# The last two output projections of a two-layer attention kernel: the earlier one set behind the last attention with factors from GpSimd, the last one as seven block products

## Chip, cores and metric

The kernel runs on one core of a Trainium2 chip. Times are device microseconds. The median of three runs is given, and one further execution, taken with the hardware profiler, is what the trace shows.

## What is computed

Two layers, each over eight images of 512 channels by 1024 positions, all in 32-bit floats. The second layer takes the first one's output.

```python
def layer(x, gn_scale, gn_bias, qkv_w, qkv_b, proj_w, proj_b):   # GROUPS is 8, then 32
    xn = group_norm(x) * gn_scale + gn_bias
    q, k, v = split(einsum('oc,bcn->bon', qkv_w, xn) + qkv_b)
    attn = softmax(einsum('bhdi,bhdj->bhij', q, k) / sqrt(64))     # 8 heads of 64
    out = einsum('bhij,bhdj->bhdi', attn, v)
    return einsum('oc,bcn->bon', proj_w, out) + proj_b + x
```

## The kernel before

**Units.** The work is cut into 16 units, one for each layer and image; the last is unit 15. A unit makes v, q and k from its normalised image `xn` (512 x 1024, kept as four tiles of 128 rows), runs attention into `ao`, and needs an output projection with residual. Order in the code is the order on each engine: nothing is moved by a scheduler.

**Block products.** Each 512 x 512 by 512 x 1024 product is done with fewer multiplications: both sides are cut into two by two blocks, and seven products of sums of blocks (numbered 1 to 7, in the order 1, 6, 2, 7, 5, 4, 3) replace eight. This is used twice over, so a product has seven outer and seven inner products, 49 pieces of 128x128 by 128x256. The sums of blocks are called factors. Those of the weights come ready from images in HBM; those of the right side are made by `Right` (L194): `mix` makes the four outer factors on VectorE (DVE), `quarter` and `single` the inner ones, on DVE or GpSimd (POOL). `left.outer(k)` is an outer factor of the weights; of block 21 only the difference with block 11 is kept in place.

**Streams.** `Stream` runs the seven inner products of an outer one: pieces on TensorE (PE) into the PSUM pairs `s0`, `s1`, `a0`, `a1`, `seed` copies between banks on ScalarE (ACT), then a `finish` on DVE and a late part (`add_late`) on POOL. The tail of one product is run inside the next (`close`). Successive products take `a0` and `a1` in turn, each with the other's `s`. `ahead` begins a second product with the first; `held` keeps a product back, and `last_two` runs it interleaved with the one behind it, so that no tail is left over. `hook` runs, behind a named product, parts that other work has put there with `at`.

**Order of a unit.** Products of v, q and k are streamed. Then, from unit 1 on, the output projection of the unit before (`project`, "the old projection") runs as a fourth stream, and then attention. Under v, q and k the last pair of the unit before is finished: sums over partitions by a DVE transposition and reduction, four small DMAs (`lt`), a reciprocal, a DMA out and two broadcast back (`rb`), a division, a bias on ACT. The inner factors of `ao` are made on DVE and POOL in the k stage (`o_part`).

**Attention.** 64 steps of scores, exponential on ACT, product with v, and a running sum of exponentials on DVE, in eight chunks. Parts for the next unit are called from `at_step`; POOL's factors there (`shadows`) follow a named sum, so that they run beside DVE operations with one input. The last unit has no next one, so its attention carries none.

**The end.** Unit 15's projection (`project_last`, L822) is not in blocks: eight groups of four matmuls of 128x512, three of each four first, then the last pair's finish and the check (`verdict`), then the fourth matmul of each group, an addition with bias and residual on DVE, and a store. The residual is loaded into `xn` under the old projection. A flag is written behind it; every engine loads it and branches past a general path that does not run here. All loads and stores here are issued by SyncE (SP), which takes them in order and waits at each for what it needs.

Of the kernel before, what the change touches and what calls it, by code (L numbers as in the profile page):

```python
# [18 lines left out]
P = 128  # L19
# [13 lines left out]
def fast_path(ctx, tc, x, qkv_wT, proj_wT, vecs, groups, out, flag):  # L33
# [43 lines left out]
    abank = [apair[i // 2][:, i % 2, :] for i in range(4)]  # L77
    turns = [t[:, i, :] for i in range(2) for t in (*sbank, *apair)]

# [61 lines left out]
    def block_rows(t, r, h):  # L141
        return t[2 * r * P : 2 * (r + 1) * P, ts(h, FD)].rearrange("(i p) n -> p i n", p=P)
# [265 lines left out]
    def run(steps):  # L408
        for step in steps:
            step()  # L410
# [200 lines left out]
    def make_pairs(stream, w, sel, bias, left, early, hook):  # L611
# [32 lines left out]
        for k in ORDER:  # L644
            if k == 1 and early is not None:
                continue

            def finish(main, m, late, k=k):
                steps[k](main, m, late)
                hook(sel, k)  # L650

            held = k == 4 and sel == "k" and w.u == 0
            stream.product(left.quarters(k), w.right.inner[k], k == 3, finish, held=held)
# [42 lines left out]

    def project(stream, w, left, hook):
        l, b = units[w.u]
# [4 lines left out]

        def load(r, h):
            room, tag = {(1, 0): (rbpool, "rb"), (0, 1): (tmppool, "tmp")}.get((r, h), (ppool, "p"))
            t = res[r, h] = room.tile([P, 2, FD], F32, tag=tag, name=f"res{r}{h}_{w.u}")
            nc.sync.dma_start(t, block_rows(src, r, h))
# [47 lines left out]
        def product(k):  # L755
            def finish(main, m, late):
                steps[k](main, m, late)
                hook("o", k)

            stream.product(left.quarters(k), w.right_o.inner[k], k == 3, finish, held=k == 4)  # L760

# [59 lines left out]

    def project_last(w, wproj, rest):  # L822
        l, b = units[w.u]
        dst = mid[b] if l == 0 else out[b]

        def products(g, c):
            o, h = divmod(g, NH)
            nc.tensor.matmul(  # L828
                turns[g], wproj[:, c, ts(o, P)], ao[:, c, ts(h, FD)],
                start=(c == 0), stop=(c == CC - 1),  # L830
            )

        for g in range(CC * NH):
            for c in range(CC - 1):
                products(g, c)
        for part in rest:
            part()
        for g in range(CC * NH):
            o, h = divmod(g, NH)
            products(g, CC - 1)  # L840
            cols = xn[:, o, ts(h, FD)]
            nc.vector.scalar_tensor_tensor(
                cols, turns[g], vec[:, l, PB, o : o + 1], cols, ALU.add, ALU.add
            )
            nc.sync.dma_start(dst[o * P : (o + 1) * P, ts(h, FD)], cols)

    def attention(w, at_step):
# [79 lines left out]
        def evacuate(c):  # L929
            pr, qh = divmod(c, NH)  # L930
            banks = banks_of(c)
            tmp = tmps[:, c % 2, :]
            if c == n_chunks - 1 and not final:
                i0 = nc.vector.tensor_copy(tmp, banks[0])
            else:
                i0 = nc.scalar.copy(tmp, banks[0])  # L936
            i1 = nc.vector.tensor_add(ao[:, pr, ts(qh, FD)], banks[1], tmp)  # L937
            state["free"][c % 2] = [i0, i1]
# [44 lines left out]
        def divide(pr):  # L983
            col = u * CC + pr
            nc.vector.scalar_tensor_tensor(
                ao[:, pr, :], ao[:, pr, :], 1.0, state["rb"], ALU.mult, ALU.mult,
                accum_out=asum[:, col : col + 1],
            )

        def add_bias(pr, h):  # L990
            cols = ao[:, pr, ts(h, FD)]
# [81 lines left out]
    for u in range(2 * B):  # L1073
        w = Unit()
        w.u, w.right, w.last, w.ready = u, right, {"v": []}, {}
        w.v = vpool.tile([P, NT, C], F32, tag="v", name=f"v_{u}")
# [4 lines left out]
        def at(sel, k, *parts):  # L1081
            hooks.setdefault((sel, k), []).extend(parts)
# [84 lines left out]
        else:  # L1167
# [15 lines left out]
            def o_part(k, lo=0, hi=4):  # L1183
                return lambda: run(o_parts[k][lo:hi])

# [33 lines left out]
        if u:  # L1219
            at("q", 1, *(partial(load_image, l, "k", 0, k) for k in ORDER))  # L1220
            lo = units[old.u][0]
            for k in ORDER:
                at("q", k, partial(load_image, lo, "o", 1, k))
        ahead = u if last else u + 1
        at("k", 5, partial(load_xn, ahead, 0, 2))
        make_pairs(stream, w, "q", QB, lefts["q"], early["q"], hook)
        if u:
            product = project(stream, old, left_slots[1], hook)
            at("k", 4, partial(old.load_res, 0, 0))
            at(  # L1230
                "k", 3, partial(load_xn, ahead, 2), partial(old.load_res, 1, 0), partial(old.load_res, 1, 1),
                partial(old.load_res, 0, 1),
            )
            at("o", 1, partial(stats_of, 0, 1))
            at("o", 2, partial(stats_of, 2, 3))
            at("o", 7, partial(stats_of, 4, 5))
            at("o", 3, partial(stats_of, 6, 7))
        else:
            at("k", 3, partial(load_xn, ahead, 2))
        make_pairs(stream, w, "k", KB, lefts["k"], early["k"], hook)  # L1240
        make = MAKE.get(u)
        if make is not None:
            at("o", 7, partial(load_raw, *make, left_slots[0]))
        if u:
            for k in ORDER:
                product(k)
        wproj = None
        if last:
            wproj = slots[0].rearrange("p k o -> p (k o)")[:, : CC * C].rearrange("p (c o) -> p c o", c=CC)
            nc.sync.dma_start(wproj, proj_wT[1].rearrange("(c p) o -> p c o", p=P))  # L1250

        right = Right(xn, xt) if not last else None
        mixing = {}
        if not last:
# [21 lines left out]
            def rest_of_high(right=right):  # L1276
                xb = ppool.tile([P, 2, FD], F32, tag="p", name=f"xb_{u + 1}")
                room, kept = halves(xb)
                run(right.quarter((2, 3), (*halves(spare), room), nc.gpsimd, kept)[1 if u == 0 else 2 :])

        making = [] if last else [None] * 8
        if make is not None:
            making = [part for parts_of in mix_left(left_slots[0]) for part in parts_of]

        def at_step(s, state):
            if nxt is None:
                return
            c, t = divmod(s, NT)
            st, stats, aggregate, means, variances, scales, apply, _ = nxt
# [323 lines left out]
```

## Time and profile before

| | us |
|---|---|
| median of three runs (lowest, highest) | 3172.73 (3171.10, 3173.76) |
| the profiled execution | 3174.36 |
| its span, first to last instruction | 3172.5 |
| PE busy in the span | 3157.8 |
| attention of unit 15 | 3028.41 to 3138.44 |
| last projection on PE | 3138.44 to 3166.10 |

The parts of a profile used here: the share of the span of each engine; the list of waits (engine and line, what it waited for, us in total, times, longest); tables of stretches with the busy time of each engine; and the timeline, with start, duration, engine, line and operation. L445 is a piece of a streamed product, L882 and L910 are scores and products of attention, L828 the last projection, L716 and L554 additions on POOL, L927 the running sums on DVE. Two instructions of PE make one matmul of 32-bit floats.

### The profile page before, as it was taken

What the parts mean: (1) busy time and instruction counts of PE and PEld (TensorE: products, weight loads), DVE (VectorE), ACT (ScalarE), POOL (GpSimd) and SP (SyncE); (2) the same over time, 40 slices, a digit from 0 to 9 for tenths busy, and PEclk for the clock granted to TensorE, in tenths of its full rate; (3) what the DMA queues carried; (4) which work ended last, traced back from release to release, by engine and by line L of the source; (5) the groups of instructions that cost most, each with busy time, mean ns of one, the idle gap of its engine ahead of it and who ended that gap; (6) DMA issues with size and microseconds to landing.
All of it is one profiled execution on the core that took longest, in us unless ns stands there. A gap on an engine that the chain in (4) does not pass through costs nothing.

```text
span 3172.5 us, 63788 instructions
## 1 busy us (share of the span) xinstructions
PE 3157.8 (100%) x24276; PEld 2023.4 (64%) x24276; DVE 2689.3 (85%) x3151; ACT 2040.3 (64%) x3572; POOL 1265.1 (40%) x966
## 2 busy tenths in 40 slices
PE   9999999999999999999999999999999999999999
PEld 7466494765847658476584756748567485674843
DVE  7988989889798897888979888798897988879777
ACT  3666767667676666766667666676666766667664
POOL 5245272452715427053361533615336162351610
PEclk9999999999999999999999999999999999999999
DMA  4334342433434324233142331423314232243311
GB/s 176 106 123 141 115 157 95 158 129 115 162 110 143 122 63 168 74 120 128 57 168 79 124 118 57 168 80 133 108 57 174 87 129 101 72 164 92 137 53 50
DMA packets 155559, 365.82 MB, mean 115 GB/s; under 512 B 30192, under 2 KB 45808, under 8 KB 155248
## 3 DMA queue, kind: packets, MB, share of 16 engines
q1 hardware_dynamic: 154528, 360.98, 34.0%
q8 instruction: 197, 3.23, 0.4%
q14 instruction: 114, 0.93, 0.1%
q10 hardware_dynamic: 720, 0.68, 0.1%
HBM read 299.72 MB, written 59.77 MB: 113 GB/s over the span
## 4 chain that ended last, share of the span: by engine, by line
PE 95%; DVE 3%; issue 1%; DMA 1%; SPq 0%; ACT 0%; POOL 0%; DVEq 0%; POOLq 0%; ACTq 0%
PE a L910 26%; PE s L882 25%; PE s L445 23%; PE a L445 17%; DVE acc L927 1%; PE a L882 1%; PE s L828 0%; PE a L828 0%; PE a L410 0%; DVE w L410 0%; DVE tr L942 0%; PE s L345 0%; PE s L410 0%; DMA lt<-red 0%; SPq L956 0%
## 5 line engine op out<-in xcount | busy, mean ns | idle before, releaser
L890 ACT ACTIVATE p<-s 128x1024 f32<-128x1024 f32 x976 | 998.1, 1024 | 516.8 <-PE s L882 490.9
L910 PE MATMUL a<-p,v 64*64 64x512 f32 x8192 | 1098.7, 589 | 0.0
L882 PE MATMUL s<-q,k 64*64 64x512 f32 x7808 | 1057.0, 590 | 1.3 <-POOL k L554 1.3
L927 DVE TENSOR_TENSOR acc<-acc,p 128x1024 f32<-128x1024 f32 x768 | 956.2, 1245 | 75.0 <-ACT p L890 33.0
L454 ACT COPY a<-s 128x256 f32<-128x256 f32 x1728 | 615.2, 358 | 345.8 <-PE s L445 246.3
L910 PEld LDWEIGHTS a<-p,v 64*64 64x64 f32 x8192 | 381.6, 131 | 497.7 <-ACT p L890 351.4
L882 PEld LDWEIGHTS s<-q,k 64*64 64x64 f32 x7808 | 380.8, 133 | 435.7 <-issue 435.7
L459 ACT COPY late<-s 128x256 f32<-128x256 f32 x432 | 161.1, 373 | 199.9 <-PE s L445 185.9
L445 PE MATMUL s<-k,w 128*128 128x256 f32 x672 | 195.2, 379 | 0.5 <-ACT a L454 0.5
L927 DVE TENSOR_TENSOR acc<-p,p 128x1024 f32<-128x1024 f32 x128 | 156.2, 1221 | 10.1 <-ACT p L890 10.1
L1327 POOL TENSOR_TENSOR k<-xn 128x256 f32<-128x256 f32 x15 | 11.0, 734 | 374.3 <-PE s L882 298.2
L942 DVE STREAM_TRANSPOSE tr<-acc 128x1024 f32<-128x1024 f32 x128 | 158.1, 1235 | 0.0
L950 DVE TENSOR_REDUCE red<-tr 128x32 f32<-128x1024 f32 x128 | 154.2, 1204 | 0.0
L445 PE MATMUL a<-xn,w 128*128 128x256 f32 x492 | 146.4, 379 | 0.0
L445 PE MATMUL a<-xt,w 128*128 128x256 f32 x462 | 137.4, 379 | 0.0
L445 PEld LDWEIGHTS s<-k,w 128*128 128x128 f32 x672 | 125.0, 190 | 19.2 <-ACT a L454 1.3
L303 POOL TENSOR_TENSOR y<-var,half 128x4 f32<-128x4 f32 (+1 forms) x17 | 18.7, 1097 | 284.7 <-DVE var L301 284.7
L937 DVE TENSOR_TENSOR ao<-a,tmp 128x512 f32<-128x512 f32 x128 | 88.1, 688 | 49.4 <-ACT tmp L936 48.8
L554 POOL TENSOR_TENSOR q<-q,late 128x512 f32<-128x512 f32 x64 | 99.4, 1553 | 63.2 <-ACT a L454 45.7
L445 PE MATMUL s<-xn,w 128*128 128x256 f32 x372 | 110.7, 379 | 0.0
L445 PE MATMUL s<-xt,w 128*128 128x256 f32 x372 | 110.6, 379 | 0.0
L563 POOL TENSOR_TENSOR v<-v,late 128x512 f32<-128x512 f32 x60 | 89.9, 1499 | 47.1 <-DVE v L665 33.9
(259 smaller groups left out, 5119.4 us busy)
## 6 DMA issues: line engine op xcount, KB each, us to landing
w<-iq SPq DMA_DIRECT2D x105, 448.0 KB, 3.5
w<-ik SPq DMA_DIRECT2D x105, 448.0 KB, 7.0
w<-io SPq DMA_DIRECT2D x105, 448.0 KB, 6.9
w<-iv SPq DMA_DIRECT2D x98, 448.0 KB, 3.7
rb<-drec SPq DMA_DIRECT2D x128, 256.0 KB, 3.8
xn<-mid SPq DMA_DIRECT2D x36, 512.0 KB, 3.6
res<-x_dram SPq DMA_DIRECT2D x32, 512.0 KB, 5.9
mid<-res SPq DMA_DIRECT2D x32, 512.0 KB, 2.8
```

What stands on the lines that cost most here:

```text
L445: nc.tensor.matmul(to, at, moving, start=start, stop=j != 1, skip_group_check=True),
L454: n = nc.scalar.copy(dst, one)
L459: on("ACT", nc.scalar.copy(late, seventh), s, 1)
L554: return nc.gpsimd.tensor_add(cols, cols, twice(late))
L563: return nc.gpsimd.tensor_add(cols, cols, parts)
L882: nc.tensor.matmul(bank[e * H : (e + 1) * H, j, :], w.k[pr][j * H : (j + 1) * H, t * P + e * H : t * P + (e + 1) * H], w.q[pr][j * H : (j ...
L890: exp = nc.scalar.activation(p, bank, AF.Exp, scale=SCALE)
L910: nc.tensor.matmul(banks[r][j * H : (j + 1) * H, :], w.v[rows, t, lo : lo + D], p[rows, j, :], start=(t == 0), stop=(t == NT - 1),)
L927: state["sums"].append(nc.vector.tensor_add(acc, state["first"] if t == 1 else acc, p))
L937: i1 = nc.vector.tensor_add(ao[:, pr, ts(qh, FD)], banks[1], tmp)
L942: nc.vector.transpose(tr, state["acc"].pop(c))
L950: nc.vector.tensor_reduce(red[:, :, qh, :], state["tr"].rearrange("p j (f i) -> p j f i", i=BL), AX.X, ALU.add)
```

## The change

Four things change, all in unit 15.

- Its old projection, that of unit 14, runs behind its attention and no longer before it. The last two products of k are interleaved instead (`held`), the first two of the moved projection are begun together (`ahead`), and its last two are no longer interleaved. The finish of unit 15's last pair hangs on the products of the moved projection.
- The inner factors of `ao` for it are made by POOL, in 16 parts at 14 steps of the last attention, in the weight slot that k has left; the parts on DVE and POOL in the k stage are dropped. Its residuals go to `xt` and `spare`.
- Unit 15's attention writes into `xn` instead of `ao`. One more DVE subtraction (`again`, 128x896) at step 3 restores a block of the weights.
- The last projection is seven outer products of four matmuls of 128x512 each, with sums on DVE, ACT and POOL. Its residuals go to q's tiles, loaded once attention is over. The flag's matmul stands before its last product.

The core of the diff; the residual load in `project`, `evacuate`, `divide` and `add_bias` change only in the tile that they name:

```diff
@@ -649,7 +648,7 @@
-            held = k == 4 and sel == "k" and w.u == 0
+            held = k == 4 and sel == "k" and w.u in (0, 2 * B - 1)
             stream.product(left.quarters(k), w.right.inner[k], k == 3, finish, held=held)
@@ -702,6 +701,10 @@
         def load(r, h):
+            if rooms is not None:
+                res[r, h] = rooms[r, h]
+                nc.sync.dma_start(res[r, h], block_rows(src, r, h))
+                return
             room, tag = {(1, 0): (rbpool, "rb"), (0, 1): (tmppool, "tmp")}.get((r, h), (ppool, "p"))
@@ -757,7 +760,11 @@
-            stream.product(left.quarters(k), w.right_o.inner[k], k == 3, finish, held=k == 4)
+            inner = w.right_o.inner
+            after = (left.quarters(6), inner[6]) if k == 1 and rooms is not None else None
+            stream.product(
+                left.quarters(k), inner[k], k == 3, finish, ahead=after, held=k == 4 and rooms is None
+            )
@@ -819,30 +826,76 @@
-    def project_last(w, wproj, rest):
+    def project_last(stream, w, left, again, rooms, rest, flagged):
...
-        dst = mid[b] if l == 0 else out[b]
-
-        def products(g, c):
-            o, h = divmod(g, NH)
-            nc.tensor.matmul(
-                turns[g], wproj[:, c, ts(o, P)], ao[:, c, ts(h, FD)],
-                start=(c == 0), stop=(c == CC - 1),
+        right = w.right_o
+        add = nc.vector.tensor_add
+        res = {}
+        for (r, h), room in rooms.items():
+            res[r, h] = room
+            nc.sync.dma_start(room, block_rows(source_of(w.u), r, h))
...
+        def steps(bank, k):
+            return [
+                partial(
+                    nc.tensor.matmul, bank[:, i, :],
+                    again[:, k - 1, :] if (c, i) == (0, 1) else left.outer(k)[:, c, ts(i, P)],
+                    right.outer[k][:, c, :], start=c == 0, stop=c == 1, skip_group_check=True,
+                )
+                for i in range(2) for c in range(2)
+            ]
...
+        def sums(name):
+            return accpool.tile([P, 2, FD], F32, tag="acc", name=f"{name}_last")
...
+        def more(r, h, t):
+            nc.gpsimd.tensor_add(res[r, h], res[r, h], t)
...
+        def store(r, h):
+            nc.sync.dma_start(block_rows(out[b], r, h), res[r, h])
...
+        first = steps(sbank[1], 1)
+        run(first[:2])
+        stream.close()
+        run(first[2:])
+        p1 = sums("p1")
+        for i in range(2):
+            nc.scalar.activation(p1[:, i, :], sbank[1][:, i, :], AF.Identity, bias=vec[:, l, PB, i : i + 1])
+        more(0, 0, p1)
+        right.mix(1)
+        run(steps(apair[0], 5))
+        right.mix(3)
+        for i in range(2):
+            for t in (res[0, 1], res[1, 1]):
+                add(t[:, i, :], apair[0][:, i, :], t[:, i, :])
+        run(steps(sbank[0], 6))
+        right.mix(2)
+        u2 = sums("u2")
+        add(u2, sbank[0], p1)
+        more(0, 1, u2)
+        run(steps(apair[1], 7))
+        u3 = sums("u3")
+        for i in range(2):
+            nc.vector.scalar_tensor_tensor(
+                u3[:, i, :], apair[1][:, i, :], step_vec[:, l, PB, i : i + 1], u2[:, i, :], ALU.add, ALU.add
...
-
-        for g in range(CC * NH):
-            for c in range(CC - 1):
-                products(g, c)
-        for part in rest:
-            part()
-        for g in range(CC * NH):
-            o, h = divmod(g, NH)
-            products(g, CC - 1)
-            cols = xn[:, o, ts(h, FD)]
-            nc.vector.scalar_tensor_tensor(
-                cols, turns[g], vec[:, l, PB, o : o + 1], cols, ALU.add, ALU.add
-            )
-            nc.sync.dma_start(dst[o * P : (o + 1) * P, ts(h, FD)], cols)
+        more(1, 0, u3)
+        more(1, 1, u3)
+        store(1, 1)
+        run(steps(sbank[1], 2))
+        add(res[0, 0], sbank[1], res[0, 0])
+        store(0, 0)
+        rest()
+        run(steps(apair[0], 4))
+        add(res[1, 0], apair[0], res[1, 0])
+        store(1, 0)
+        flagged(apair[1])
+        run(steps(sbank[0], 3))
+        for i in range(2):
+            t = res[0, 1][:, i, :]
+            add(t, sbank[0][:, i, :], t)
+            nc.sync.dma_start(out[b][i * P : (i + 1) * P, FD:], t)
@@ -930,11 +983,11 @@
             tmp = tmps[:, c % 2, :]
-            if c == n_chunks - 1 and not final:
+            if c == n_chunks - 1:
                 i0 = nc.vector.tensor_copy(tmp, banks[0])
...
                 i0 = nc.scalar.copy(tmp, banks[0])
-            i1 = nc.vector.tensor_add(ao[:, pr, ts(qh, FD)], banks[1], tmp)
+            i1 = nc.vector.tensor_add(w.ao[:, pr, ts(qh, FD)], banks[1], tmp)
             state["free"][c % 2] = [i0, i1]
@@ -1023,12 +1076,10 @@
-        if final:
-            run([partial(add_bias, CC - 2, h) for h in range(NH)] + w.sums)
         w.finish = [partial(reciprocals, CC - 1), partial(divide, CC - 1)]
...
         w.before = [partial(divide, CC - 2), *(partial(add_bias, CC - 2, h) for h in range(NH))]
-        w.right_o = Right(ao, ot)
+        w.right_o = Right(w.ao, ot if not final else w.v[:, :6, :].rearrange("p (a b) o -> p a b o", b=2))
@@ -1181,13 +1232,13 @@
             def o_part(k, lo=0, hi=4):
-                return lambda: run(o_parts[k][lo:hi])
+                return lambda: run(o_parts[k][lo:hi]) if not last else None
...
             at("v", 4, reciprocals, bias_2[0])
-            at("v", 3, bias_2[1], o_rooms, partial(ro.mix, 0))
+            at("v", 3, bias_2[1], *(() if last else (o_rooms,)), partial(ro.mix, 0))
             at("q", 6, divide)
@@ -1221,14 +1272,19 @@
                 at("q", k, partial(load_image, lo, "o", 1, k))
-        ahead = u if last else u + 1
-        at("k", 5, partial(load_xn, ahead, 0, 2))
+        if not last:
+            at("k", 5, partial(load_xn, u + 1, 0, 2))
         make_pairs(stream, w, "q", QB, lefts["q"], early["q"], hook)
-        if u:
+        if last:
+            places = [(0, 0), (0, 1), (1, 0), (1, 1)]
+            product = project(
+                stream, old, left_slots[1], hook, dict(zip(places, (*(xt[:, i] for i in range(3)), spare)))
+            )
+        elif u:
             product = project(stream, old, left_slots[1], hook)
...
             at(
-                "k", 3, partial(load_xn, ahead, 2), partial(old.load_res, 1, 0), partial(old.load_res, 1, 1),
+                "k", 3, partial(load_xn, u + 1, 2), partial(old.load_res, 1, 0), partial(old.load_res, 1, 1),
                 partial(old.load_res, 0, 1),
@@ -1236,18 +1292,14 @@
         else:
-            at("k", 3, partial(load_xn, ahead, 2))
+            at("k", 3, partial(load_xn, u + 1, 2))
         make_pairs(stream, w, "k", KB, lefts["k"], early["k"], hook)
...
             at("o", 7, partial(load_raw, *make, left_slots[0]))
-        if u:
+        if u and not last:
             for k in ORDER:
                 product(k)
-        wproj = None
-        if last:
-            wproj = slots[0].rearrange("p k o -> p (k o)")[:, : CC * C].rearrange("p (c o) -> p c o", c=CC)
-            nc.sync.dma_start(wproj, proj_wT[1].rearrange("(c p) o -> p c o", p=P))
@@ -1278,14 +1330,39 @@
+        else:
...
+            w.ao = xn
+            room = slots[0].rearrange("p k o -> p (k o)")
+            wide = [room[:, i * FD : (i + 1) * FD].rearrange("p (i n) -> p i n", i=2) for i in range(9)]
+            narrow = [room[:, i * FD2 : (i + 1) * FD2].rearrange("p (i n) -> p i n", i=1) for i in range(18, 21)]
+            again = room[:, 21 * FD2 : 21 * FD2 + 7 * P].rearrange("p (k o) -> p k o", k=7)
+            ro = old.right_o
+            fives, fours = (
+                ro.quarter(pair, rooms, nc.gpsimd)
+                for pair, rooms in (((5, 6), wide[3:6]), ((4,), narrow))
+            )
+            wides = [*ro.quarter((1, 7), wide[:3], nc.gpsimd), *fives, *ro.quarter((2, 3), wide[6:], nc.gpsimd)]
+            places = (8, 10, 16, 18, 24, 26, 32, 34, 40, 42, 48, 50)
+            shadows = {s: [part] for s, part in zip(places, wides)}
+            shadows[56], shadows[58] = fours[:3], fours[3:]
+            for r in range(2):
+                for h in range(2):
+                    old.load_res(r, h)
...
         making = [] if last else [None] * 8
...
         def at_step(s, state):
+            c, t = divmod(s, NT)
             if nxt is None:
+                for part in shadows.get(s, ()):
+                    follows(part(), state["sums"][-1 if t == 0 else -2], "beside operations with one input")
+                if s == 3:
+                    quarters = (left_slots[1].block[:, :, i : i + P] for i in (0, P))
+                    nc.vector.tensor_sub(again, *quarters)
                 return
-            c, t = divmod(s, NT)
             st, stats, aggregate, means, variances, scales, apply, _ = nxt
@@ -1344,9 +1421,24 @@
-    project_last(old, wproj, [*old.finish, verdict])
-    nc.tensor.matmul(turns[0][:1, :1], both, ones[:, :1], start=True, stop=True)
-    nc.scalar.copy(flag, turns[0][:1, :1])
...
+    (reciprocals, divide, *bias), (transposed, reduced), (_, *bias_2) = w.finish, w.sums, w.before
+    at("o", 1, transposed, bias_2[0])
+    at("o", 6, reduced, bias_2[1])
+    at("o", 2, partial(w.right_o.mix, 0))
+    at("o", 7, reciprocals)
+    at("o", 3, divide, *bias)
...
+    def flagged(bank):
+        nc.tensor.matmul(bank[:1, 0, :1], both, ones[:, :1], start=True, stop=True)
+        nc.scalar.copy(flag, bank[:1, 0, :1])
...
+    for k in ORDER:
+        product(k)
+    project_last(
+        stream, w, left_slots[1], again,
+        {(r, h): q_pairs[r][:, :, ts(h, FD)] for r in range(2) for h in range(2)}, verdict, flagged,
+    )
```

More of the change, by code (lines that the diff above doesn't have):

```diff
@@ L77, in fast_path @@
     abank = [apair[i // 2][:, i % 2, :] for i in range(4)]
-    turns = [t[:, i, :] for i in range(2) for t in (*sbank, *apair)]
     vec = const.tile([P, 2, 6, CC], F32, name="vec")
@@ L695, in stream_values, with project @@
             stream.product(left.quarters(k), w.right.inner[k], k == 3, finish, True, after)
-    def project(stream, w, left, hook):
+    def project(stream, w, left, hook, rooms=None):
         l, b = units[w.u]
@@ L985, in divide @@
             nc.vector.scalar_tensor_tensor(
-                ao[:, pr, :], ao[:, pr, :], 1.0, state["rb"], ALU.mult, ALU.mult,
+                w.ao[:, pr, :], w.ao[:, pr, :], 1.0, state["rb"], ALU.mult, ALU.mult,
                 accum_out=asum[:, col : col + 1],
@@ L990, in add_bias @@
         def add_bias(pr, h):
-            cols = ao[:, pr, ts(h, FD)]
+            cols = w.ao[:, pr, ts(h, FD)]
             nc.scalar.activation(
@@ L1074, in fast_path @@
         w = Unit()
-        w.u, w.right, w.last, w.ready = u, right, {"v": []}, {}
+        w.u, w.right, w.last, w.ready, w.ao = u, right, {"v": []}, {}, ao
         w.v = vpool.tile([P, NT, C], F32, tag="v", name=f"v_{u}")
```

## The prediction

> **What bounds the kernel now.** I read the share of the span per engine first, then the engine's waits, then a table of stretches, then the timeline around the two seams that the change opens. TensorE (PE) is busy 3157.8 us of the 3172.5 us span at full granted clock, and its waits are few:
>
> ```profile
> PE 3157.8 (100%) x24276; PEld 2023.4 (64%) x24276; DVE 2689.3 (85%) x3151; ACT 2040.3 (64%) x3572; POOL 1265.1 (40%) x966
> PE s L445 <- ACT a L454: 2.2, 3, 1.3
> PE s L882 <- POOL k L554: 1.3, 1, 1.3
> ```
>
> So a gain must come from fewer matmuls or a shorter end, and a loss from a new wait of PE or a longer end. The stretches below are the attention of the last but one unit, that of the last, the old projection before it, the last projection, and what follows PE (columns: length, then busy time of PE, weight loads, DVE, ACT, POOL, then clock, DMA share, GB/s):
>
> ```profile
> 2832.33:2942.59 110.26, 110.26 (x1033) 49.89 (x1032) 98.49 (x114) 76.45 (x84) 17.80 (x18) 1.00 0.28 89
> 3028.41:3138.44 110.03, 110.03 (x1026) 40.49 (x1025) 94.19 (x97) 71.11 (x76) 3.23 (x3) 1.00 0.13 41
> 3006.00:3028.40 22.40, 22.40 (x104) 19.25 (x102) 12.99 (x15) 13.35 (x38) 18.83 (x12) 1.00 0.36 129
> 3138.44:3166.10 27.66, 27.66 (x68) 12.07 (x64) 14.77 (x26) 3.15 (x5) 0.00 (x0) 1.00 0.20 68
> 3166.10:3172.50 6.40, 0.19 (x3) 0.09 (x2) 0.75 (x2) 0.15 (x1) 0.00 (x0) 0.83 0.38 136
> ```
>
> PE never stops in the first four. The last pair's chain (sums, four small DMAs, reciprocal, broadcast, division, bias: 3138.4 to 3158.5) fits under three quarters of the last projection. After PE come a DVE addition, a store of 2.0 us, and about 3 us of ending.
>
> **The change, part by part.** (1) *Matmuls.* A matmul is two instructions here. The old projection, 49 products of 128x256 at 0.4315 us (3006.18, 3006.61, 3007.04 in the timeline), is 21.14 us and only moves. The last one has 32 matmuls of 128x512, 64 instructions at 0.4295 us (the chain's 5.15 us for 12), 27.49 us; seven products of four are 28 matmuls, 24.05 us: **-3.44 us**.
>
> (2) *Attention now starts behind the last two products of k, interleaved.* Unit 0 already starts so, and pays twice: 1.33 us on PE at 81.85 (ACT waits for DVE, which is behind with three weight factors), and 1.31 us at 91.76, where the fifth score step waits for POOL's late addition, itself behind a 3.00 us factor at L1086. Neither factor is there in the last unit, whose o-part factors also leave DVE and POOL in the k stage. DVE's last k addition should end 1.4 us after PE, POOL's 2.7 us after; the third step needs the one at 1.7 us, the fifth the other at 5.3 us. One thing is new: 21 products run before this attention instead of 28, so the first scores write the very bank that the last product's ACT copies still read. In the old order that last copy runs 3028.14 to 3028.50 against the first scores at 3028.41. I take **+0.30**; bounds 0 and unit 0's 2.64.
>
> (3) *Factors by POOL inside attention.* Twelve subtractions of 128x512 (1.28 us, rows of L1327) and four of 128x256 (0.73 us): 18.3 us, and one DVE subtraction of 128x896 (1.08 us). The last attention has 110.03 - 94.19 = 15.84 us of DVE idle. The last but one attention holds 17.80 us of POOL work placed the same way, and is only 0.23 us longer, with seven extra PE instructions. I take **+0.05**; bounds 0 and 0.23, with every factor's time added to DVE as a rival below.
>
> [...]
>
> ```profile
> 2971.47 1.22 DVE L587 TENSOR_TENSOR u_q<-a,p_q 128x1024 f32<-128x1024 f32 x1 [1.67 <-ACT a L454]
> 2972.61 1.22 DVE L985 SCALAR_TENSOR_TENSOR ao<-ao,rb 128x1024 f32<-128x1024 f32 x1
> 2972.77 2.19 POOL L554 TENSOR_TENSOR u_q<-u_q,late 128x512 f32<-128x512 f32 x1 [3.85 <-DVE u_q L587]
> ```
>
> DVE keeps its 1.22 us, POOL goes from 1.27 to 2.19.
>
> (4) *Old projection behind attention.* Set t = 0 where attention's last matmul ends. The seam is the one that ends every other unit's attention, where PE goes on without a listed wait: 0. PE finishes at t = 21.1, plus two matmuls of the last projection run before the old one's tail (1.7): its last product ends at 22.9. DVE meanwhile: evacuation and two sums to 3.9 (as after 2942.66), p1 4.5-5.9, transpose to 7.1, u2 8.3, reduction 9.5, product 2's addition 10.9, one factor 12.1, u3 14.1, reciprocal 15.9, four additions of product 5 to 18.4, product 4 to 20.0, product 3 23.1-24.3. The small DMAs land 3.7 us after the reduction (3144.8 to 3148.5), 13.2, before they are asked for; the broadcast lands 5.9 us after the reciprocal (3149.96 to 3155.89), 21.5, before the division: no wait. Division 25.5, two ACT biases (1.33) 26.9, factor 6 (1.22) 28.1.
>
> (5) *Last projection.* PE ends product 1 at 24.6 and product 5 at 28.06; product 6 needs factor 6, so **+0.15**. The flag's small matmul comes before the last product: **+0.20**, both ends near it (0.19 in the old order). PE ends at 21.14 + 24.05 + 0.35 = 45.54, where it ended at 27.66. Attention ends 21.14 - 0.35 = 20.79 us earlier, so PE ends 20.79 + 27.66 - 45.54 = **2.91 us earlier**.
>
> (6) *SP's queue.* The residuals of the last unit, once loaded under attention, go into q's tiles, and their issue stands behind the old projection's stores. SP waits in order, so it waits for POOL:
>
> ```profile
> SPq L719 <- POOL res L554: 180.5, 45, 10.8
> 3022.59 2.37 POOL L716 TENSOR_TENSOR res<-res,u_o 128x1024 f32<-128x1024 f32 x1
> 3008.08 1.41 SPq L707 DMA_DIRECT2D res<-mid  x3
> 3011.00:3014.00 3.00, 3.00 (x16) 2.63 (x15) 1.33 (x3) 1.80 (x5) 1.98 (x2) 1.00 0.96 352
> 3162.00:3164.00 2.00, 2.00 (x6) 0.90 (x5) 1.79 (x3) 0.00 (x0) 0.00 (x0) 1.00 0.84 327
> ```
>
> POOL has, behind each other, four additions of 2.36 us and six of 1.27 us; from p1 on it runs 5.9, 8.3, 9.6, 12.0, 13.2; then 14.1-17.7; then from product 5's end 18.4-22.0, and product 4's late part at 23.3-23.6. So four loads of 512 KB are issued from 23.7 at 0.45 us each. With one store ahead, 2.6 MB at the 352 GB/s above take 7.4 us from 24.9: the last lands at X = 32.3. DVE needs that block for product 5's four additions (0.68 each; the first needs an earlier block): 34.4, then factor 4 (35.6) and u2 (36.8). POOL then adds u2 and twice u3, three times 2.31 us: 43.75. Only then does SP issue the first of five last stores, and the other four stand behind it. 2.1 MB at 327/0.84 = 389 GB/s is 5.4 us, plus 1.6 us until landing (256 KB lands in 2.0, 512 KB in 2.8): 50.8. Without that queue the last half block would land 3.35 us after PE (0.1 + 0.69 + 0.35 + 2.0, as before: 3166.10 to 3169.3 is 3.2), at 48.9. **+1.9 us.** The loads hide under product 5 to 7; if that cover is gone, the verdict on DVE (8.6 us behind X) comes after the flag's matmul wants it at 42.0, that is from X = 33.4, and PE waits too.
>
> **Sum:** -2.91 + 1.9 - 0.05 (the last addition and store, 3.15 for 3.2) = **-1.06 us**: span 3171.4. The profiled execution took 3174.36 us, 1.86 beyond its span and 1.63 above the median of the runs shown, 3172.73; I keep both offsets, so the median becomes **3171.7 us**. Its own range, X between 31 and 33.3, is 3170.4 to 3172.8.
>
> **Rivals.** *The end stays short* (X at 30 or earlier, POOL prompt): the queue's 1.9 us vanish, -2.9, 3169.8. For it: stores alone land in 2.0 us. Against: seven ordered waits. *Late residuals, the slower side:* X moves one for one into the end; from X = 33.3 the gain is gone. [...] For it: DVE is fuller here than in the old place (division, reduction, factors between). Against: DVE's PSUM reads, most of this stage, left POOL at 1.27 and 2.36. *Unit 0's start repeats:* 2.64 for 0.30, 3174.0; against it, both causes are absent. *Factors collide with sums:* +3.5 by the idle account (18.3 + 1.08 - 15.84), 3175.2; against it stands the neighbouring attention. *It does not shorten the work:* the counts show four matmuls fewer, so this needs a wait that I have not found.
>
> **Chances.** Forecast 0.45, short end 0.20, late residuals 0.17, unit 0's start 0.05, collisions 0.06, an unseen wait 0.07. The range 3169.0 to 3177.3 leaves out the unseen wait and a few hundredths below. A difference of 0.2% is 6.3 us, about what a measurement of this kernel tells from no change. Faster by that needs twice the matmuls saved: 0.02. Slower by that needs over 7 us beyond the sum, the unseen wait or a late chain past its bound: 0.08. Within: 0.90.
>
> **What would show it.** Right: 28 matmuls at L409 at 0.86 us each, no wait of PE over 0.5 us, POOL's factors beside attention of 110.0 to 110.3 us, the old projection 21 us, and stores bunched after PE ends. Wrong: PE waiting at the first five score steps, at L444 behind ACT or DVE, or at L409 for a factor; residuals of the last unit landing before t = 30 or after 34; a last store landing within 3.4 us of PE's end.

## The result, and the profile after

| | before | after |
|---|---|---|
| median (lowest, highest) of 20 runs each, us | 3172.61 (3170.79, 3173.86) | 3177.57 (3175.34, 3178.83) |
| the profiled execution, us | 3174.36 | 3177.55 |
| its span, us | 3172.5 | 3175.7 |
| from the start of unit 15's products of v to the end, us | 229.91 | 235.04 |

The change costs 4.96 us: a ratio of 1.0014, 95% interval 1.0008 to 1.0021. By the medians that is +0.16%, under the 0.2% named above, yet the interval leaves 1 out. The last row of the table compares the two profiles without the two microseconds by which their earlier, unchanged parts differ: 3172.5 - 2942.59 and 3175.7 - 2940.66, **+5.13 us**. All later lengths of "unit 15 to the end" are made in this way, from one profiled execution each.

Engines and PE's waits after:

```profile
PE 3155.9 (99%) x24268; PEld 2027.9 (64%) x24268; DVE 2693.6 (85%) x3152; ACT 2039.7 (64%) x3573; POOL 1283.5 (40%) x978
PE s L344 <- DMA xn<-x_dram: 4.6, 1, 4.6
PE a L1433 <- DVE both L1422: 4.3, 1, 4.3
PE s L444 <- ACT a L453: 2.2, 3, 1.3
PE s L935 <- POOL k L553: 1.3, 1, 1.3
```

Eight instructions of PE (four matmuls) are gone, and one wait is new: the flag's matmul (L1433) waits 4.3 us for DVE. The 4.6 us before the first matmul of the program (L344) stand in the kernel before too, which the prediction's list leaves out. The stretches, with columns as before: unit 15's attention; the old projection with six of the seven last products; the wait; the flag's matmul with the last product; what follows PE.

```profile
3005.51:3115.54 110.03, 110.03 (x1025) 46.27 (x1025) 96.32 (x98) 70.95 (x75) 20.95 (x18) 1.00 0.08 24
...
3115.54:3157.81 42.27, 42.27 (x150) 27.54 (x146) 31.62 (x38) 16.07 (x41) 24.76 (x13) 1.00 0.34 113
3157.81:3162.12 4.31, 0.00 (x1) 0.00 (x1) 4.17 (x8) 0.00 (x0) 3.40 (x2) 0.93 0.00 0
3162.12:3168.97 6.85, 6.85 (x10) 2.60 (x10) 1.09 (x1) 0.15 (x1) 0.00 (x0) 0.54 0.61 233
3168.97:3175.70 6.73, 0.00 (x0) 0.00 (x0) 1.29 (x2) 0.00 (x0) 0.00 (x0) 0.71 0.24 86
```

Attention takes 110.03 us as before, now with 20.95 us of POOL beside it. PE is full until the flag. Then it waits for 4.31 us, and the flag and last product take 6.85 us at a clock of 0.54, where the same work takes 0.20 + 3.44 at full clock: 3.2 us more. So +5.13 is made of -2.7 (the work saved on PE, much as predicted), +4.3, +3.2 and +0.3 (6.73 for 6.40 behind PE). The clock in finer stretches:

```profile
3158.00:3162.00 4.00, 0.00 (x0) 0.00 (x0) 3.86 (x8) 0.00 (x0) 3.21 (x2) 0.94 0.00 0
...
3162.00:3164.00 2.00, 1.88 (x4) 0.92 (x5) 1.21 (x2) 0.15 (x1) 0.00 (x0) 0.50 0.96 373
3164.00:3166.00 2.00, 2.00 (x4) 0.86 (x3) 0.00 (x0) 0.00 (x0) 0.00 (x0) 0.50 0.98 377
3166.00:3168.00 2.00, 2.00 (x4) 0.82 (x3) 0.00 (x0) 0.00 (x0) 0.00 (x0) 0.50 0.13 49
3168.00:3170.00 2.00, 0.97 (x2) 0.00 (x0) 0.99 (x2) 0.00 (x0) 0.00 (x0) 0.91 0.00 0
3170.00:3172.00 2.00, 0.00 (x0) 0.00 (x0) 0.30 (x1) 0.00 (x0) 0.00 (x0) 0.95 0.41 152
```

A mean of 0.94 over 4 us, taken as 1.00 and then the 0.50 of the next rows, is 0.12 x 4 = 0.48 us at half clock: by this estimate the fall is at 3161.5, 3.7 us after PE stopped at 3157.81. From then on PE is at 0.50 until 3168.4, although it works again from 3162.1. By the same sum the clock falls once more at 3171.8, behind the last product.

What the flag waited for, the verdict (its operations at L1416 to L1422), is in the timeline of DVE and POOL:

```profile
3146.76 0.69 DVE L871 TENSOR_TENSOR q<-a,q 128x512 f32<-128x512 f32 x1 [1.87 <-DMA q<-mid]
3150.03 1.89 DVE L871 TENSOR_TENSOR q<-a,q 128x512 f32<-128x512 f32 x3 [2.58 <-DMA q<-mid]
...
3154.26 6.96 POOL L853 TENSOR_TENSOR q<-q,u_last 128x1024 f32<-128x1024 f32 x3 [6.37 <-DVE u_last L875]
...
3155.64 1.21 DVE L887 TENSOR_TENSOR q<-s,q 128x1024 f32<-128x1024 f32 x1
3156.77 2.20 DVE L1416 TENSOR_SCALAR fin<-asum 128x64 f32<-128x64 f32 x1
3159.00 0.22 DVE L1418 TENSOR_REDUCE low<-fin 128x1 f32<-128x64 f32 x1
3159.14 2.12 DVE L1420 TENSOR_SCALAR extremes<-extremes 128x64 f32<-128x64 f32 x1
3161.30 0.22 DVE L1421 TENSOR_REDUCE low<-extremes 128x1 f32<-128x64 f32 x1
3161.44 0.18 DVE L1420 TENSOR_SCALAR extremes<-extremes 128x64 f32<-128x64 f32 x1
```

In the kernel before, the whole verdict takes 1.35 us, 3157.16 to 3158.51:

```profile
3157.16 0.20 DVE L1339 TENSOR_SCALAR fin<-asum 128x64 f32<-128x64 f32 x1
...
3157.53 0.18 DVE L1343 TENSOR_SCALAR extremes<-extremes 128x64 f32<-128x64 f32 x1
...
3158.36 0.15 DVE L1345 TENSOR_REDUCE both<-low 128x1 f32<-128x3 f32 x1
```

In the changed kernel DVE waits twice for the residuals (1.87 and 2.58 us), and the verdict's first operation starts at 3156.77, 1.0 us before PE wants the flag. That operation takes 0.20 us in the kernel before and 2.20 us here; the same operation on `extremes` takes 2.12 us and then, with POOL done, 0.18 us. POOL's three additions of 2.32 us end at about 3156.6, 3158.9 and 3161.2; the two slow operations end at 3158.97 and 3161.26. The reductions between them keep 0.22 us.

### The profile page after: what moved, and what is told of

Read it like the earlier page. It is cut to its first block, busy times and chain, and to the rows that moved or that the text cites. A ratio compares the mean times of both kernels' runs of the same rounds, so it can differ in the third digit from the quotient of the medians.

```text
span 3175.7 us, 63791 instructions
## 1 busy us (share of the span) xinstructions
PE 3155.9 (99%) x24268; PEld 2027.9 (64%) x24268; DVE 2693.6 (85%) x3152; ACT 2039.7 (64%) x3573; POOL 1283.5 (40%) x978
## 4 chain that ended last, share of the span: by engine, by line
PE 97%; DVE 2%; DMA 1%; issue 0%; ACT 0%; POOL 0%; SPq 0%; ACTq 0%; DVEq 0%; POOLq 0%
PE a L963 27%; PE s L935 26%; PE s L444 23%; PE a L444 17%; PE a L935 1%; PE s L409 1%; DVE acc L980 0%; PE a L409 0%; DMA q<-mid 0%; DVE w L409 0%; DMA gmat<-groups_dram 0%; DMA rb<-drec 0%; PE s L344 0%; DMA drec<-rec 0%; POOL k L553 0%
## 5 line engine op out<-in xcount | busy, mean ns | idle before, releaser
L553 POOL TENSOR_TENSOR k<-k,late 128x512 f32<-128x512 f32 x64 | 100.0, 1563 | 23.6 <-DVE k L624 11.7
```

The costliest lines, as they stand in the source:

```text
L553: return nc.gpsimd.tensor_add(cols, cols, twice(late))
```

## Experiments

The theory to be tested: three prices in a chain. Late residuals push the verdict into the time in which POOL adds; POOL's additions stop the verdict's small operations; PE's idle time then lowers its clock. The rivals: the queue of stores behind POOL would set the end in any case; or the moved projection itself costs time. Each median is given beside that of the kernel before on the same chip; the first four ran on one chip, the next four on another, the last two on a third. The changed kernel was not measured again beside them, and each interval reaches 2 to 3 us to either side, so a difference of medians from its 3177.57 is rough; the lengths from unit 15 to the end say where the time lies.

**1. The flag behind the last product.**

```diff
+        run(steps(sbank[0], 3))
         flagged(apair[1])
-        run(steps(sbank[0], 3))
```

> The flag's matmul stands behind the last block product instead of before it; nothing else. Theory (late verdict: TensorE waits 4.3 us for the check on VectorE, and comes out of the wait at half its granted clock, so that the last product takes 6.7 us for 3.4): no wait of TensorE over 0.5 us, clock 1.00 through the last product, and 4.5 to 7.5 us less than the changed kernel's 3177.6, about 3172. Rival 1 (the queue of stores at the end binds whatever TensorE does): 3176 or more. Rival 2 (the clock falls at the end by itself): the 4.3 us go, the slow product stays, about 3173.3 with clock 0.5.

Measured: 3175.68 us against 3172.3, ratio 1.0009 (0.9999 to 1.0018), unit 15 to the end 232.29. The wait no longer stands before a product (1.28 us of it are left behind the last one) and the last product runs at full speed. But 1.9 us of the median and 2.75 of the profile came back, where 4.5 to 7.5 were expected. Last product, stores, and two stretches with the DMA's share and rate in the last two columns:

```profile
3158.60 3.60 PE L409 MATMUL s<-xn,w 128*128 128x512 f32 x8
...
3162.60 2.37 SPq L856 DMA_DIRECT2D out_dram<-q  x3
...
3166.31 0.86 SPq L898 DMA_DIRECT2D out_dram<-q  x2
```

```profile
3163.90:3164.90 1.00, 0.00 (x0) 0.00 (x0) 1.00 (x2) 0.01 (x1) 0.00 (x0) 1.00 1.07 410
...
3166.90:3167.90 1.00, 0.00 (x0) 0.00 (x0) 0.00 (x0) 0.00 (x0) 0.00 (x0) 0.50 1.03 381
```

The last product ends at 3162.2 and the span at 3173.9, 11.7 us later instead of the 6.4 of the kernel before. The first three stores are issued from 3162.6, when POOL is done, and fill the DMA engines (share 1.03 to 1.07); the last two stand behind them and land 4.8 us after their issue, for 3.0 in the changed kernel. So the queue that the prediction described is real and is the next limit, but in the changed kernel it is hidden under the slow last product.

**2. The verdict early**, behind the division, before the residuals matter.

```diff
-        rest()
...
-    at("o", 3, divide, *bias)
+    at("o", 3, divide, *bias, verdict)
```

> The check on VectorE stands right behind the last division, where VectorE would wait for ScalarE's biases, instead of behind product 2's addition. Theory: its seven operations take about 1.4 us there, TensorE does not wait at the flag, clock 1.00, about 3172 to 3173 (the stores still stand behind GpSimd's three last additions). Rival (the check is slowed wherever GpSimd adds, and factor 6 is late instead): 3 to 4 us of waiting at product 6, 3176 to 3178.

Measured: 3173.84 us against 3172.3, ratio 1.0006 (0.9997 to 1.0015); 231.50, between the two expectations. The flag waits for nothing. The new place has a POOL addition too, and the verdict pays there:

```profile
3139.21 2.18 POOL L553 TENSOR_TENSOR xt<-xt,late 128x512 f32<-128x512 f32 x1 [0.82 <-DVE xt L715]
...
3140.31 1.14 DVE L1415 TENSOR_SCALAR fin<-asum 128x64 f32<-128x64 f32 x1
```

The operation ends as POOL's does (3141.45 and 3141.39). Factor 6 comes later by this, and PE waits 0.8 us for it at product 6. The stores still stand behind POOL (first issue at 3160.67), so the residuals keep a price without the verdict.

**3. The residuals early**: the same four loads, issued before the moved projection's products and so ahead of its stores in SP's queue. q's tiles are free from there on.

```diff
-            nc.sync.dma_start(room, block_rows(source_of(w.u), r, h))
...
+    rooms = {(r, h): q_pairs[r][:, :, ts(h, FD)] for r in range(2) for h in range(2)}
+    for (r, h), room in rooms.items():
+        nc.sync.dma_start(room, block_rows(source_of(w.u), r, h))
     for k in ORDER:
         product(k)
...
```

> The last unit's four residual loads are issued before the old projection's products, so that they do not stand behind its stores in SyncE's queue. Theory (late residuals start the chain): the loads land some 25 us earlier, product 5's additions wait for no DMA, the check ends about 3 to 4 us earlier, the first of the last stores goes out 4 us earlier; TensorE waits at the flag for under 1.5 us; 3169.5 to 3172. Rival (the check's operations, held up by GpSimd's additions, are enough alone): the wait at the flag is still over 2 us with a fallen clock, 3174 or more.

Measured: 3171.70 us against 3172.3, ratio 0.9999 (0.9990 to 1.0008); 228.71. As expected: against the changed kernel, 5.9 us of median and 6.3 us of profile come back by the place of four loads.

```profile
3145.84 2.48 DVE L870 TENSOR_TENSOR q<-a,q 128x512 f32<-128x512 f32 x4
...
3156.59 1.73 DVE L1415 TENSOR_SCALAR fin<-asum 128x64 f32<-128x64 f32 x1
3158.30 0.89 SPq L855 DMA_DIRECT2D out_dram<-q  x2
```

DVE's four additions of product 5 run without a wait for a DMA. The verdict still meets POOL (1.73 us), but PE waits only 0.69 us and the clock stays at 1.00.

**4. Five matmuls to fill the wait**, into the other half of the flag's bank, before the flag; their result is not used.

```diff
+        for _ in range(5):
+            nc.tensor.matmul(
+                bank[:, 1, :], left_slots[1].outer(3)[:, 0, :P], w.right_o.outer[3][:, 0, :],
+                start=True, stop=True,
+            )
         nc.tensor.matmul(bank[:1, 0, :1], both, ones[:, :1], start=True, stop=True)
```

> Five matmuls of 128x512 into a free bank (4.3 us of work, result unused) before the flag's matmul fill the time in which TensorE waited. Theory (the wait is what lowers the clock): the clock stays 1.00, the last product takes 3.4 us, 3.3 us less than the changed kernel, about 3174.2. Rival (the clock falls for another reason): the last product takes 6.7 us as before, 3177 to 3178.

Measured: 3175.72 us against 3172.3, ratio 1.0011 (1.0002 to 1.0020); 232.75. With useless work the median is 1.85 us under the changed kernel's, which the intervals do not tell apart; the profile, of the fastest of eleven runs, is 2.29 us shorter. PE's idle time before the flag is 0.54 us, and:

```profile
3161.24 0.19 PE L1438 MATMUL a<-ones,both 128*1 128x1 f32 x2 [0.54 <-DVE both L1422]
3161.36 3.70 PE L409 MATMUL s<-xn,w 128*128 128x512 f32 x8
...
3163.00:3165.00 2.00, 2.00 (x5) 0.57 (x3) 0.00 (x0) 0.00 (x0) 0.00 (x0) 1.00 1.05 407
```

The last product starts when the verdict lets it, as in the changed kernel, but at full clock: the flag and the product take 3.82 us (3161.24 to 3165.06) for 6.85. With the wait filled the clock stays at 1.00, and with PE idle for 4.31 us it fell to 0.50: it was the idleness that lowered it here. Of these 3.03 us, 0.53 are lost because the flag comes that much later in this execution, its residuals landing 0.5 us later behind attention, and 0.2 lie behind PE (6.94 us to the end for 6.73).

**5. What 1 to 4 point to**: residuals early as in experiment 3, the verdict between product 5's additions and factor 4, where POOL is idle, and the store of block (1,1) behind that of (0,0).

```diff
         run(steps(sbank[0], 6))
+        rest()
         right.mix(2)
...
-        store(1, 1)
         run(steps(sbank[1], 2))
         add(res[0, 0], sbank[1], res[0, 0])
         store(0, 0)
-        rest()
+        store(1, 1)
```

> Early residual loads as in the third run, the check on VectorE between product 5's additions and factor 4, where GpSimd has nothing to add, and the store of block (1,1) behind that of (0,0). Theory: the check takes about 1.4 us, TensorE waits nowhere over 0.3 us, clock 1.00, and the saving of matmuls shows at last: 2 to 3 us under the kernel before, 3169.5 to 3170.5. Rival (something else at the end still binds, such as GpSimd's additions or the stores): 3171.5 or more, no gain on the third run's 3171.7.

Measured: 3171.24 us against 3173.49, ratio 0.9994 (0.9985 to 1.0003); 227.54, or 2.37 below the kernel before. That is the 2 to 3 us expected, though not the 3169.5 to 3170.5, since the kernel before took longer on this chip. PE no longer waits at the flag, and all of the verdict's operations take their short time:

```profile
3148.71 0.18 DVE L1415 TENSOR_SCALAR fin<-asum 128x64 f32<-128x64 f32 x1
...
3149.06 0.19 DVE L1419 TENSOR_SCALAR extremes<-extremes 128x64 f32<-128x64 f32 x1
```

**6. The move alone**: the moved projection and POOL's factors stay, with early residuals; the last projection is that of the kernel before, 32 matmuls, with its weights loaded where k's products were.

```diff
-    def project_last(stream, w, left, again, rooms, rest, flagged):
+    def project_last(stream, w, wproj, rooms, rest):
...
+        for g in range(CC * NH):
+            for c in range(CC - 1):
+                products(g, c)
+            if g == 0:
+                stream.close()
+                rest()
```

> The move alone: the old projection behind attention with GpSimd's factors, but the last projection as the 32 matmuls of the kernel before, with its check and flag at their old places, its weights and residuals loaded right behind attention. Theory (the move costs nothing, the block form of the last projection brought both the saving and the waits): within 1 us of the kernel before, 3171.5 to 3173.3, no wait of TensorE over 0.5 us. Rival (the move itself costs, through factors on GpSimd or the last pair's chain): 3174 or more, with the wait in the old projection or behind it.

Measured: 3172.08 us against 3173.49, ratio 0.9995 (0.9986 to 1.0004); 230.11 against 229.91. PE has no wait in the moved part, and the whole is 0.2 us longer in the profile: that is what the move and POOL's factors cost.

**7. POOL's last two additions behind the verdict**, the rest as changed. This tests the stop itself.

```diff
-        more(1, 0, u3)
-        more(1, 1, u3)
-        store(1, 1)
...
-        rest()
+        checked = rest()
+        follows(more(1, 0, u3), checked, "behind the check")
+        more(1, 1, u3)
+        store(1, 1)
```

> As the changed kernel, but GpSimd's last two additions come behind the check, so that the check's two slow operations (2.2 and 2.1 us) have no GpSimd operation beside them. Theory (they stand still until a GpSimd addition ends): each takes 0.2 us, the check ends about 4 us earlier, the wait at the flag falls from 4.3 to under 1 us and the clock stays 1.00; the last two stores are later by some 2 us, so 3174 to 3176.5 in all. Rival (they are slow for another reason, say a first use or the operand): 2 us each as before, wait over 3 us, 3178 or more.

Measured: 3174.66 us against 3173.49, ratio 1.0006 (0.9997 to 1.0015); 233.80.

```profile
3156.91 0.18 DVE L1416 TENSOR_SCALAR fin<-asum 128x64 f32<-128x64 f32 x1
3157.03 9.39 SPq L856 DMA_DIRECT2D out_dram<-q  x3
...
3157.27 0.18 DVE L1420 TENSOR_SCALAR extremes<-extremes 128x64 f32<-128x64 f32 x1
```

With the residuals as late as before and the same operations in the same place, 2.20 and 2.12 us become 0.18 and 0.18: POOL's additions were the cause. PE waits 0.86 us instead of 4.31 and keeps its clock (3.70 us for the last product). The additions are only put off, the issue of the three stores takes 9.4 us (SP waits between them), and most of the gain goes back to the end.

**8. Two filling matmuls in place of five.** The diff is that of the fourth, with `range(2)`.

> As the run with the filled wait, but two matmuls in place of five, so that about 2.6 us of the wait remain. Theory (a wait lowers the clock only past some 3 us): the clock stays 1.00 and the last product takes 3.4 to 3.6 us. Rival (any wait near 2 us lowers it): clock 0.5 and over 5 us for the last product.

Measured in a single execution: 3176.04 us; 234.28. The clock fell and the last product took 5.40 us, against the expectation; but the wait came out at 3.05 us and not at 2.6, so the run shows that 3.05 us can be enough, and does not decide between the theory's "some 3 us" and the rival's "near 2".

```profile
3161.84 0.19 PE L1438 MATMUL a<-ones,both 128*1 128x1 f32 x2 [3.05 <-DVE both L1422]
...
3161.97 5.40 PE L409 MATMUL s<-xn,w 128*128 128x512 f32 x8
...
3162.00:3163.00 1.00, 1.00 (x4) 0.60 (x3) 0.94 (x1) 0.15 (x1) 0.00 (x0) 0.74 1.04 403
3163.00:3164.00 1.00, 1.00 (x2) 0.34 (x1) 0.00 (x0) 0.00 (x0) 0.00 (x0) 0.50 1.06 410
3164.00:3165.00 1.00, 1.00 (x2) 0.34 (x1) 0.00 (x0) 0.00 (x0) 0.00 (x0) 0.50 1.04 399
3165.00:3166.00 1.00, 1.00 (x3) 0.42 (x2) 0.00 (x0) 0.00 (x0) 0.00 (x0) 0.56 0.85 326
```

By the same sum as above (0.74 is 0.52 us at half clock, 0.56 is 0.88 us) the clock is low from 3162.5 to 3165.9, 3.4 us, and it falls 0.6 us after PE has begun to work again.

**9 and 10. The fifth kernel again, and with its last product in two banks**, so that the first half's addition and store need not wait for the second half.

```diff
-        run(steps(sbank[0], 3))
-        for i in range(2):
+        run(steps(sbank[0], 3)[:2])
+        run(steps(apair[1], 3)[2:])
+        for i, bank in enumerate((sbank[0], apair[1])):
             t = res[0, 1][:, i, :]
-            add(t, sbank[0][:, i, :], t)
+            add(t, bank[:, i, :], t)
```

> The fifth run's kernel (early residuals, early check, reordered store), with the second half of the last product in a PSUM pair of its own, so that the addition and the store of its first half need not wait for the second. Theory (VectorE waited for the whole pair): the first addition runs beside the last two matmuls, one addition and one store are left behind TensorE's end, 0.5 to 1.5 us under the fifth run on the same chip, 0.08 to 0.12% under the kernel before. Rival (the end is set by the store's landing and the ending alone): within 0.3 us of the fifth run.

> The fifth run's kernel once more, for the comparison on the same chip and for a second estimate against the kernel before: 1.5 to 3 us under it. If it is within 0.5 us or above it, the gain seen in the fifth run was chance.

Measured, against 3172.91: in two banks 3169.44 us, ratio 0.9992 (0.9983 to 1.0001), 227.12; the fifth kernel again 3171.40, ratio 0.9994 (0.9985 to 1.0003), 227.57. The last additions, first in one bank (experiment 5), then in two:

```profile
3163.10 1.29 DVE L896 TENSOR_TENSOR q<-s,q 128x512 f32<-128x512 f32 x2 [2.46 <-PE s L409]
```

```profile
3159.01 0.69 DVE L897 TENSOR_TENSOR q<-s,q 128x512 f32<-128x512 f32 x1 [0.74 <-PE s L409]
...
3160.79 0.69 DVE L897 TENSOR_TENSOR q<-a,q 128x512 f32<-128x512 f32 x1 [1.09 <-PEq L1652]
```

The first half's addition now runs 1.8 us before the second's. In the profiles it is worth 0.45 us, in the medians 1.96; with the runs overlapping (3168.73 to 3171.66 and 3169.13 to 3172.35) its size is open. All three comparisons of these kernels lie 1.5 to 3.5 us under the kernel before, and each interval still touches 1: a gain is likely and not proved.

## Why the prediction was wrong

The forecast was 3171.7 us and the result 3177.57, 0.27 us beyond the range. The step that failed is the last sentence of part (6): "the verdict on DVE (8.6 us behind X) comes after the flag's matmul wants it at 42.0, that is from X = 33.4, and PE waits too." The condition was right, and the sum took it as not met, at X = 32.3. Both of its sizes were off, and one consequence was missing:

- *X was 34.5, not 32.3.* The issue was near its forecast: the store of (1,0) at t = 23.75 (23.6), the loads behind it from 24.2 (23.7). The landing was not. The sum let one store of 512 KB share the engines, at 352 GB/s; the loads shared them with three, issued at 3138.06, 3139.29 and, behind the loads, 3142.28, and all moved at 266 to 334 GB/s:

```profile
3139.78 2.37 SPq L837 DMA_DIRECT2D q<-mid  x4
...
3142.00:3146.00 4.00, 4.00 (x10) 1.57 (x9) 2.36 (x2) 1.65 (x3) 0.71 (x2) 1.00 0.95 266
3146.00:3150.00 4.00, 4.00 (x11) 1.78 (x10) 0.69 (x1) 0.00 (x0) 1.89 (x1) 1.00 0.94 334
```

- *The 8.6 us were 12.0* (3162.07 for the verdict's end, less 3115.54 and 34.5). In the kernel before, where POOL has nothing to do, the verdict takes 1.35 us; here it took 5.3, and no term of the sum has that. The prediction had in hand a row in which POOL pays beside DVE (2.19 us for 1.27), and no term of its sum lets DVE pay beside POOL. In that row POOL starts later (2972.77, DVE's division at 2972.61); here it is the verdict's first operation that starts later (3156.77, POOL's second addition at 3156.58), and DVE pays. One input was no shelter: that operation has one, and took 2.20 us beside POOL's addition and 0.18 without it (experiment 7). With X at 34.5 and 8.6 us the wait would have been 34.5 + 8.6 - 42.3 = 0.8 us; with 12.0 it was 4.3.
- *The fall of the clock was in no term:* 3.2 us, shown by experiment 4. No row of the kernel before has such a wait inside the work, so none gave its price. The fall itself was in the prediction's own table: 3166.10:3172.50, with PE idle from 3166.29, has a mean clock of 0.83, that is 2.2 us at half clock, from 3170.3.

Of the rivals, *late residuals* named the right place and the right chain. The range's upper end, 3177.3, allows for 0.92 us more in each of POOL's six late additions of the moved projection, a term that no run shows: in the changed kernel two of them took 2.26 and 2.18 us, the other four 1.26 to 1.28, and X came to 34.5. Nor does X move "one for one into the end": it was 2.2 us beyond the sum, and the profile 6.2 us (+5.13 for -1.06), most of it by the verdict's slow operations beside POOL and by the clock. That the upper end comes so near the measured time is chance.

The other steps:

- (1) to (5) held. PE saved 2.7 us of the predicted 2.91. Attention took 110.03 us, the flag was wanted at t = 42.3 (42.0), and at the seam before attention the first scores start 0.71 us after the last piece's start, where it was 0.52: +0.19 for +0.30. With the verdict out of the way all of it is visible: experiment 5 is 2.37 us shorter in the profile.
- (3) held against its rival: attention with the factors takes the same 110.03 us, and the whole move costs 0.2 us (experiment 6).
- (6), the store queue, +1.9: the mechanism is real (experiment 1) and sets the end once PE does not; in the changed kernel it was covered, for three stores had landed by 3166.4 while PE worked at half clock. Its price has a slip: 0.1 + 0.69 + 0.35 + 2.0 is 3.14, not 3.35, which makes it +2.1 and the forecast 3171.9.
- Of the signs set down, "no wait of PE over 0.5 us" stood for being right and failed; "residuals of the last unit landing before t = 30 or after 34" stood for being wrong and was met, at 34.5.

## What to carry to other kernels

In a queue that waits in order, a load whose room is free belongs ahead of the stores that wait for other engines; here the place of four loads was worth 6 us. The verdict's 0.18 us operations of 128x64 on DVE took, where they met an addition of POOL, whatever that addition had left, up to 2.22 us, so price such an operation from the place that it is moved to, not from the one that it leaves. And a wait of TensorE may go on costing when it is over: here 4.3 us of it cost 3.2 us more and 3.05 us cost 1.7 (5.40 for 3.70), and in the profile five useless matmuls were cheaper.

## What the hardware showed that was not expected

- A DVE operation of 128x64 with one input, 0.18 us alone, took 1.14 to 2.22 us beside a POOL addition. It ended with that addition each time (3158.97 for about 3158.9, 3161.26 for about 3161.2, 3141.45 for 3141.39). Reductions of the same tile kept 0.22 us. A subtraction of 128x1024 with two inputs, 1.22 us elsewhere, lost in the same way in the moved projection: 2.37 us at 3126.58, behind a POOL addition that ends at 3127.86. What the two engines contend for is not in the traces.
- The granted clock fell to 0.50 in a wait of 4.31 us and behind one of 3.05. It stayed there for 6.9 us in the one and 3.4 us in the other, near a ratio of two, though PE was busy again after 0.6 us in the first and before the fall in the second. Both falls came 3.7 us after PE's last matmul, but that is no fixed delay: it was 2.8 us at the end of the changed kernel (3168.97 to 3171.8) and 4.0 at the end of the kernel before (3166.29 to 3170.3). The changes of the clock were at 3161.5, 3168.4 and 3171.8 in the changed kernel, 6.9 and 3.4 us apart, and at 3162.5 and 3165.9 in experiment 8, 3.4 us apart. Whether what a wait costs hangs on when it comes as well as on its length is open: no run here varied either alone. Waits of 0.54, 0.69, 0.82, 0.86 and 1.28 us did not lower the clock, nor did those of 1.3 us in unit 0 (1.00 from 78 to 98 us of the kernel before); for the 4.6 us before the program's first matmul the profile gives 1.00 throughout. Where between 1.33 and 3.05 us the limit lies, if it is one, was not tried.
- Stores alone moved up to 410 GB/s over 1 us (experiments 1 and 8); 389 GB/s had been worked out from the kernel before.
